# Feature rows beside a group's first tile, a shorter rest before the gates, and another order of the last two groups in a two-layer graph network

## The chip, the cores and the metric

The kernel runs on one core of a Trainium2 chip. The metric is the device time of one execution in microseconds; before the change the median of three runs is 2276.93 us (2276.39 to 2278.49).

The core has five engines with a queue of instructions each, worked through in order: PE (matrix multiplication; PEld are its weight loads), DVE (vector), ACT (scalar and table functions), POOL and SP. In this kernel POOL issues the indirect transfers (gathers and scatters by a list of row numbers), SP and ACT the direct ones.

## The reference

A graph of 6250 nodes with 256 features and 106250 edges, sorted by target, goes through two layers. Each layer adds its result to its input and normalizes the sum.

```python
# layer 0: two small networks, one per kind of edge, on the source's features
h = relu(x[src] @ W_rel[r].T + b_rel[r]); msg = relu(h @ W_rel[r].T + b_rel[r])
agg = segment_sum(msg, dst)
i, f, g, o = split(agg @ W_ih.T + b_ih + b_hh, 4)
hn = sigmoid(o) * tanh(sigmoid(i) * tanh(g))
x = layernorm(x + relu(relu(hn @ W1.T + b1) @ W2.T + b2) @ W3.T + b3)

# layer 1: attention over the incoming edges, four heads of 64; self loops are added to the edges
h = x @ W
e = leaky_relu(a_src[src] + a_dst[dst], 0.2)
alpha = softmax of e over the edges of each target
y = segment_sum(h[src] * alpha, dst) + bias + x
x = layernorm(x + relu(layernorm(y) * gamma + beta))
```

Since the two networks of layer 0 depend on the source node and the kind of edge alone, the kernel computes them once per node and kind and gathers the results.

## The kernel before

**Prologue.** The edge lists are packed so that the self loops fall out, 100000 edges stay and every tile holds 128 of them, 782 tiles (`TC`) in all. Seven tiles make a window, 112 of them (`NW`), which covers at most 64 neighbouring target nodes; two windows make a group, 56 of them (`NG`), whose 128 slots (64 per window) lie on the 128 partitions. The first node of a window is read into SP registers (`lows_of`). The last two windows of the list have no room for 64 whole rows behind their first node, so group 55 moves its own rows by an indirect transfer with the row numbers `tail_x` (reading) or `tail_i` (writing). Both are derived from `tail` (L1105 to L1117), where slots of window 110 that belong to window 111 get a row number outside the nodes, the same for all of them. Then the message networks run (PE, DVE's L1165, ACT's L1168) and their rows are stored in `parts0`.

**Layer 0** (`fast`, first half). A loop over `n` works through the tiles: POOL gathers the 128 message rows of tile `n` (L1646, recorded at L1265 in the helper `gather`), and PE sums tile `n - 4` into the group's accumulator with a one-hot matrix (`sum0`, L1622). With the first tile of a group SP loads the group's self-loop messages (`own_rows`, L1423; a gather on POOL for group 55). Work after the sums is cut into chains, Python generators in `Steps`. After each tile, `run.step()` lets every chain whose rest is over issue its next piece, the older chain first; a `yield k` rests for `k` tiles, a `yield 0` is a `yield 1`. After the last tile `run.finish()` steps until all chains are through. So the rests decide the order in which instructions stand in the engines' queues.

Two chains belong to a group's end. `turn` adds the self loops on DVE (L1433, L1437) and one step later transposes the sums into `faT` (PE L1448, DVE L1451). `update` runs once for four groups, for two near the end, and singly for groups 52 to 55. Its pieces: SP loads the groups' feature rows `xn` (L1461; for group 55 a POOL gather), rest 4, six gate pieces (PE L1475, ACT L1483), tanh (ACT L1492), `hn` (DVE L1495), three layers (L1499 with L1503, L1506 with L1508 and the bias added to `xn` at L1511, L1520 with the residual `xn` at L1522), the normalization (ACT L1529, a square root, which needs another table in ACT than the gates; DVE L1531, L1536), transposition (L1545, L1549), the product with the second layer's weights (PE L1558, ACT L1562 and L1563) and the store into `rows1` (SP L1569; for group 55 the POOL scatter L1571).

**Layer 1** (second half) can gather from `rows1` only when all of it is stored. Its loop over `t` gathers tile `t` (L1930). Per group, `weights` computes the attention scores: a transposition (PE L1750), scans over the edges (DVE L1757, L1758), a product (PE L1761, L1762), two more scans (L1767, L1768), a transposition (PE L1773), and on DVE L1776 to L1779 with ACT's exponential into `ex` (L1781). It then puts the group's pieces into the list `late`: the two windows, and for all groups but 55 one more tile that is shared with the next group. `sum1` takes a piece from `late`, weights its rows on DVE (`weighted`: L1796, ACT L1801, L1802; ahead of a group's first piece the one-hot matrix, L1348), and issues one sum on PE (L1911). In the loop it is called once or twice per tile, from `t = 782` on twice. When a group's sums are issued, the chain `finish` divides and normalizes: DVE L1817 to L1827, L1834 to L1841, then twice the pieces of `normed` (DVE L1849, L1850, ACT L1851, L1852, DVE L1854, ACT L1857), with DVE L1861 to L1863 between. SP stores the rows (L1868), two halves per group, each after the earlier one has landed; group 55 uses the POOL scatter L1870.

Buffers are handed out in rotation by `ring(pool, shape, dtype, name, n)`, `n` being their number.

Of the kernel before, what the change touches and what calls it, by code (L numbers as in the profile page):

```python
# [33 lines left out]
F32 = mybir.dt.float32  # L34
I32 = mybir.dt.int32
AF = mybir.ActivationFunctionType
OP = mybir.AluOpType
# [5 lines left out]
P = 128  # L43
N = 6250
D = 256
# [658 lines left out]
def gnn_kernel(  # L704
# [67 lines left out]
    with (  # L772
# [15 lines left out]
        with (  # L788
# [260 lines left out]
            for to, of in (  # L1049
# [55 lines left out]
            tail = lp.tile([P, 2], F32, name="tail")  # L1105
            lo, hi = slice(0, SLOTS), slice(SLOTS, P)
            nc.vector.tensor_add(tail[lo, 0:1], iota_p[lo], low_b[lo, NW - 2 : NW - 1])
            nc.vector.tensor_scalar(
                tail[lo, 1:2], tail[lo, 0:1], low_b[lo, NW - 1 : NW], float(NP), op0=OP.is_ge, op1=OP.mult
            )  # L1110
            nc.vector.tensor_tensor(tail[lo, 0:1], tail[lo, 0:1], tail[lo, 1:2], op=OP.max)
            nc.vector.scalar_tensor_tensor(
# [83 lines left out]
def fast(  # L1196
# [50 lines left out]
    def windows_of(g):  # L1247
        return range(2 * g, 2 * g + 2)

    def lows_of(ws):  # L1250

        ws = [w for w in ws if w < NW - 2]
        return dict(zip(ws, lows(ws[0], len(ws)))) if ws else {}
# [83 lines left out]
    def ring(pool, shape, dtype, name, n):  # L1337

        of = rings.setdefault((name, id(pool)), [[], 0])
        if len(of[0]) < n:  # L1340
            of[0].append(pool.tile(shape, dtype, name=f"{name}_{len(of[0])}"))
        of[1] += 1
        return of[0][(of[1] - 1) % n]
# [17 lines left out]
    with (  # L1361
# [64 lines left out]

        def turn(g, i, ps, aT):

            agg = ring(up, [P, D], F32, "agg", 3)

            kind = ring(up, [P, 2], F32, "kind", 3)
            for r in range(2):
                nc.vector.tensor_scalar(  # L1433
                    kind[:, r : r + 1], ps[:, D:], float(3 - r), None, op0=OP.is_equal
                )
            for r, of in ((0, ps[:, :D]), (1, agg)):
                nc.vector.scalar_tensor_tensor(  # L1437
                    agg,
                    loop0[g][:, r * D : (r + 1) * D],
                    kind[:, r : r + 1],  # L1440
                    of,
                    op0=OP.mult,
                    op1=OP.add,
                )
            yield 1
            pt = ring(upp, [P, 4 * P], F32, "fpg", 5)[:, : 2 * P]
            for k in range(2):
                nc.tensor.transpose(  # L1448
                    pt[:, k * P : (k + 1) * P], agg[:, k * P : (k + 1) * P], ident
                )  # L1450
            nc.vector.tensor_copy(  # L1451
                aT[:, :, i * P : (i + 1) * P], pt.rearrange("p (k n) -> p k n", k=2)
            )

        def update(groups, aT):
            slow = min(3, max(1, (NG - 4 - groups[0]) // 4))
            cols = len(groups) * P
            at_w = lows_of([w for g in groups for w in windows_of(g)])
            xn = [ring(up, [P, D], F32, "fxn", 8) for g in groups]
            for i, g in enumerate(groups):  # L1460
                own_rows(g, at_w, xn[i], x)  # L1461
            yield 4
            hn = ring(up, [P, 2, 4 * P], F32, "fhn", 2)
            cells = []
            for m in range(2):
# [131 lines left out]
                        nd3[half_of(w), :, :, :].rearrange("p c a h -> p c (a h)"),  # L1597
                    )

        got, ohs, sums, turned, stored, loop0 = {}, {}, {}, {}, [], {}  # L1600
        run.start(weights_of_logits())

        def order_of(g):
# [29 lines left out]
        for n in range(TC + LAG):  # L1633
            if n < TC:
                g, t = order[n]
                k, turns = n % WT, n // WT // 10 % 2
                if k == 0:
                    seven = ring(rowsp, [P, WT * HA], F32, "G", 10).rearrange(
                        "p (j f) -> p j f", f=HA
                    )  # L1640
                    m = min(WT, TC - n)
                    of, to = mark[:, n : n + m, None], seven[:, :, D : D + 1]
                    nc.scalar.copy(to[:, ::-1, :][:, :m, :] if turns else to[:, :m, :], of)

                got[t] = seven[:, WT - 1 - k if turns else k, : D + 1]
                gather(got[t][:, :D], parts0, idx0[:, t : t + 1])  # L1646
                if t == order_of(g)[0]:
                    ohs[g] = ring(ep, [P, 2 * W8, SLOTS], F32, "oh0", 2)
                    one_hot(ohs[g], 2 * g, 2 * W8)
                    loop0[g] = ring(up, [P, 2 * D], F32, "loop0", 2)  # L1650
                    own_rows(g, lows_of(windows_of(g)), loop0[g], loops)
            if n >= LAG:
                g, t = order[n - LAG]
                if t != 2 * WT * g:
                    sum0(g, t, t == TC - 1)
                elif g:
                    sum0(g - 1, t, True)
                if t == 2 * WT * g + WT:
                    sum0(g, 2 * WT * g)
            run.step()  # L1660
# [3 lines left out]
    with (  # L1664
# [72 lines left out]
        def weights(pair, box):  # L1737
# [45 lines left out]
            for i, g in enumerate(pair):  # L1783

                for w in reversed(windows_of(g)):
                    late.append((g, w, i * GS + WT * (w % 2), len(tiles_of(w)[0]), G[w], ex, by(top)))
                if g < NG - 1:
                    late.append((g, w + 2, i * GS + 2 * WT, 1, G[w + 2], ex, by(top)))

        def weighted(g, w, o, n, of, ex, top):  # L1790
# [88 lines left out]
        pair_of = {g: p for p in pairs for g in p}  # L1879
        boxes = {p[0]: {} for p in pairs}  # L1880
        sums, queue, read, ohs, k3s, left, written = {}, [], set(), {}, {}, {}, []

        def sum1():

# [38 lines left out]
        while t < TC + LAG or late or queue or run.chains:  # L1923
            if t < TC:
                w = t // WT
                if t % WT == 0:
                    G[w] = ring(rowsp, [P, WT * HA], F32, "G", 10).rearrange(
                        "p (j f) -> p j f", f=HA
                    )
                gather(G[w][:, t - WT * w, :], rows1, idx1[:, t : t + 1])  # L1930
            k = t - LAG
            if 0 <= k < TC:
                w = k // WT
                g = w // 2
                pair = pair_of[g]
                box = boxes[pair[0]]
                if k % (2 * WT) == 0:
                    if g == pair[0]:
                        box["e"] = ring(ep, [P, 2 * GS, H], F32, "e", 3)
                    if g:  # L1940

                        old = pair_of[g - 1]
                        ob = boxes[old[0]]
                        nc.scalar.copy(  # L1944
                            ob["e"][:, old.index(g - 1) * GS + 2 * WT, :], G[w][:, 0, D:HA]
                        )
                        if old is not pair:
                            run.start(weights(old, ob))
                if k == tiles_of(w)[0][-1]:
                    o = pair.index(g) * GS + WT * (w % 2)  # L1950
                    own = len(tiles_of(w)[0])
                    nc.scalar.copy(box["e"][:, o : o + own, :], G[w][:, :own, D:HA])
                    if w == NW - 1:
                        run.start(weights(pair, box))
            sum1()
            if len(queue) + W8 * len(late) > 3 * W8 or t % 7 == 0 or t >= TC:
                sum1()
            run.step()
            t += 1

# [61 lines left out]
```

## Time and profile before

| what | us |
|---|---|
| median of three runs | 2276.93 |
| the profiled execution | 2273.88 |
| its span, first to last instruction | 2271.7 |
| first gather of layer 0 | 203.70 |
| last gather of layer 0 | 1190.38 |
| first gather of layer 1 | 1220.96 |
| last gather of layer 1 | 2205.13 |
| last scatter | 2259.47 |
| busy: PE, DVE, ACT, POOL | 1550.3, 1235.5, 506.9, 1526.7 |

A row of the timeline has the start and the duration in us, the engine, the line, the operation, what it writes and reads, how often, and in brackets how long the engine had been idle and what ended that. A row of a group has its number of instructions, busy time and mean duration in ns, and the idle time ahead of them by what ended it. "q" behind an engine's name stands for its queue (issuing a transfer, waiting for a semaphore).

### The profile page before, as it was taken

To read this page: it belongs to the slowest core of one execution; us is meant where nothing else is said; L and a number is where in the kernel's file an instruction comes from. 1 tells how busy PE (TensorE), PEld (TensorE's weight loads), DVE (VectorE), ACT (ScalarE), POOL (GpSimd) and SP (SyncE) were. 2 spreads that over 40 slices of the span, in tenths; PEclk is the share of its full clock that TensorE was granted. 3 is DMA by queue.
4 is the path that set the end of the run, shared out by engine and by line. 5 is a ranking of instruction groups with operands and counts; after the bars stand their busy time and mean duration, and the time that the engine had idled before them with its cause. 6 is when DMAs were issued, how large, how long until landed. Compare 5 with 4: busy or idle time off the path is not lost. (4 is left out here: it accounts for less than half of the span.)

```text
span 2271.7 us, 22029 instructions
## 1 busy us (share of the span) xinstructions
PE 1550.3 (68%) x5722; PEld 769.7 (34%) x5722; DVE 1235.5 (54%) x3332; ACT 506.9 (22%) x1525; POOL 1526.7 (67%) x1603
## 2 busy tenths in 40 slices
PE   8987688888988888888992354554545555355564
PEld 5654233333333333333451232322323223232232
DVE  7452133333333343333542577677776877777786
ACT  3322022221222212222342112211111111212111
POOL 1213777777777777777774777777777777777760
PEclk9988899999999999999996676766767666676776
DMA  5335435554555555555553555555555555555550
GB/s 160 123 95 152 132 115 168 165 159 144 144 168 165 157 149 144 168 164 164 172 163 93 143 156 149 155 144 158 151 147 162 144 157 151 148 160 146 151 145 24
DMA packets 163393, 332.53 MB, mean 146 GB/s; under 512 B 42451, under 2 KB 74290, under 8 KB 163257
## 3 DMA queue, kind: packets, MB, share of 16 engines
q0 software_dynamic: 75968, 208.00, 33.9%
q1 hardware_dynamic: 64736, 82.92, 11.4%
q10 hardware_dynamic: 22553, 40.12, 5.8%
q8 instruction: 47, 0.77, 0.1%
q14 instruction: 89, 0.73, 0.1%
HBM read 278.79 MB, written 52.12 MB: 146 GB/s over the span
## 5 line engine op out<-in xcount | busy, mean ns | idle before, releaser
L1265 POOL DMA_INDIRECT G<-parts,fidx x782 | 748.5, 957 | 305.7 <-issue 218.4
L1265 POOL DMA_INDIRECT G<-rows,fidx x782 | 747.3, 956 | 240.6 <-issue 221.1
L1622 PE MATMUL fps<-G,oh 128*64 128x257 f32 (+1 forms) x1674 | 523.4, 425 | 149.2 <-DMA G<-parts,fidx 142.4
L1911 PE MATMUL fps<-gw,oh 128*64 128x264 f32 (+1 forms) x1674 | 440.0, 475 | 230.8 <-DVE gw L1802 230.6
L1911 PEld LDWEIGHTS fps<-gw,oh 128*64 128x64 f32 (+1 forms) x1674 | 231.3, 169 | 408.8 <-DVE gw L1802 247.6
L1622 PEld LDWEIGHTS fps<-G,oh 128*64 128x64 f32 (+1 forms) x1674 | 191.9, 147 | 457.4 <-DMA G<-parts,fidx 241.5
L1802 DVE TENSOR_TENSOR gw<-G,bank 128x1792 f32<-128x1792 f32 (+1 forms) x167 | 248.9, 1490 | 178.0 <-ACT gw L1801 174.9
L1433 DVE TENSOR_SCALAR kind<-fps 128x1 f32<-128x1 f32 x112 | 12.5, 152 | 308.5 <-PE fps L1622 308.5
L1475 PE MATMUL fpg<-faT,fWihT 128*128 128x512 f32 (+2 forms) x432 | 172.4, 524 | 0.0
L1750 PE MATMUL turn<-fident,e 128*120 128x128 f32 (+2 forms) x30 | 13.7, 457 | 223.6 <-ACT e L1944 223.6
L1348 DVE TENSOR_TENSOR oh<-bank,fslot 128x1024 f32<-128x1024 f32 x112 | 135.9, 1213 | 2.2 <-ACT bank L1781 2.2
L1583 DVE COPY nd<-hr 128x4 f32<-128x4 f32 x56 | 10.9, 194 | 162.6 <-ACT hr L1562 162.6
L1851 ACT ACTIVATE frs<-fmv,eps_c 128x1 f32<-128x1 f32 x112 | 33.0, 294 | 297.0 <-DVE fmv L1850 147.1
L1143 PE MATMUL fph<-fxc,fWrT 128*128 128x512 f32 (+1 forms) x208 | 92.7, 595 | 6.5 <-DMA fWrT<-in_WrT_dram 6.4
L1475 PEld LDWEIGHTS fpg<-faT,fWihT 128*128 128x128 f32 x432 | 72.1, 194 | 68.8 <-issue 58.9
L931 POOL DMA_INDIRECT packed<-frame,place x21 | 20.9, 993 | 108.2 <-DVE fms L1165 70.8
L1857 ACT ACTIVATE fy<-fy,frs 128x256 f32<-128x256 f32 x112 | 67.2, 600 | 100.2 <-DVE gw L1796 55.1
L1157 PE MATMUL fpm<-fWrT,fhT 128*128 128x256 f32 x392 | 89.0, 380 | 0.6 <-DVE fms L1165 0.5
L1750 PEld LDWEIGHTS turn<-fident,e 128*120 128x120 f32 (+2 forms) x30 | 5.0, 168 | 238.0 <-ACT e L1944 236.0
L1801 ACT COPY gw<-bank 128x28 f32<-128x28 f32 (+1 forms) x167 | 28.4, 170 | 228.5 <-DMA dB<-slots 101.3
L1157 PEld LDWEIGHTS fpm<-fWrT,fhT 128*128 128x128 f32 x392 | 73.3, 190 | 17.7 <-issue 5.0
L1165 DVE TENSOR_TENSOR fms<-fpm,fbrr 128x512 f32<-128x512 f32 x49 | 33.6, 687 | 76.1 <-PE fpm L1157 74.9
(236 smaller groups left out, 1817.8 us busy)
## 6 DMA issues: line engine op xcount, KB each, us to landing
kept<-keep SPq DMA_DIRECT2D x56, 384.0 KB
k<-kept ACTq DMA_DIRECT2D x56, 384.0 KB
dB<-slots ACTq DMA_DIRECT2D x112, 128.0 KB
loop<-parts SPq DMA_DIRECT2D x110, 128.0 KB
parts<-fms SPq DMA_DIRECT2D x49, 256.0 KB
G<-parts,fidx POOLq DMA_INDIRECT x782
G<-rows,fidx POOLq DMA_INDIRECT x782
rows<-hr SPq DMA_DIRECT2D x110, 65.0 KB
```

The lines of the kernel that those rows point to most:

```text
L1143: nc.tensor.matmul(ph[:, :cols], WrT_s[:, r, k, m * P : (m + 1) * P], xc[:, k, :cols], start=(k == 0), stop=(k == 1),)
L1157: nc.tensor.matmul(pm[:, r, :], hT[:, r, k, j * P : (j + 1) * P], WrT_s[:, r, k, :], start=(k == 0), stop=(k == 1),)
L1165: nc.vector.tensor_add(ms.rearrange("p r f -> p (r f)"), pm.rearrange("p r f -> p (r f)"), brr)
L1265: nc.gpsimd.indirect_dma_start(out=to_tile, out_offset=None, in_=table, in_offset=bass.IndirectOffsetOnAxis(ap=idx, axis=0),)
L1348: nc.vector.tensor_tensor(to[:, :nj, :], iota_s[:, None, :].to_broadcast([P, nj, SLOTS]), of[:, :, None].to_broadcast([P, nj, SLOTS]), op= ...
L1475: nc.tensor.matmul(pg[:, :cols], WihT_s[:, k, c * P : (c + 1) * P], aT[:, k, :cols], start=(k == 0), stop=(k == 1),)
L1622: nc.tensor.matmul(sums[g][to, :], ohj, got[t], start=begins, stop=ends)
L1801: nc.scalar.copy(gw[:, :, D:HA], ex[:, o : o + n, :])
L1802: nc.vector.tensor_mul(gw[:, :, :D].rearrange("p j (h f) -> p j h f", h=H), of[:, :n, :D].rearrange("p j (h f) -> p j h f", h=H), ex[:, o ...
L1851: nc.scalar.activation(r, mv[u, k, 1:2], AF.Ln, bias=eps_c[u])
L1857: nc.scalar.activation(y, y, AF.Identity, bias=m, scale=r)
L1911: nc.tensor.matmul(sums[g][to, :], ohj, gw, start=begins, stop=ends)
```

## The change

```diff
             nc.vector.tensor_add(tail[lo, 0:1], iota_p[lo], low_b[lo, NW - 2 : NW - 1])
-            nc.vector.tensor_scalar(
-                tail[lo, 1:2], tail[lo, 0:1], low_b[lo, NW - 1 : NW], float(NP), op0=OP.is_ge, op1=OP.mult
+            nc.vector.tensor_scalar(tail[lo, 1:2], iota_p[lo], float(NP + SLOTS), None, op0=OP.add)
+            nc.vector.scalar_tensor_tensor(
+                tail[lo, 1:2],
+                tail[lo, 0:1],
+                low_b[lo, NW - 1 : NW],
+                tail[lo, 1:2],
+                op0=OP.is_ge,
+                op1=OP.mult,
             )
...
         def turn(g, i, ps, aT):
-            agg = ring(up, [P, D], F32, "agg", 3)
+            agg = ring(up, [P, D], F32, "agg", 2)
...
         def update(groups, aT):
...
-            xn = [ring(up, [P, D], F32, "fxn", 8) for g in groups]
-            for i, g in enumerate(groups):
-                own_rows(g, at_w, xn[i], x)
-            yield 4
+            xn = [rows_x[g] for g in groups]
+            yield 2
...
                     loop0[g] = ring(up, [P, 2 * D], F32, "loop0", 2)
-                    own_rows(g, lows_of(windows_of(g)), loop0[g], loops)
+                    rows_x[g] = ring(up, [P, D], F32, "fxn", 9)
+                    at_w = lows_of(windows_of(g))
+                    own_rows(g, at_w, loop0[g], loops)
+                    own_rows(g, at_w, rows_x[g], x)
...
         def weights(pair, box):
...
-                if g < NG - 1:
+                if g == NG - 1:
+                    weighed.append(g)
+                else:
                     late.append((g, w + 2, i * GS + 2 * WT, 1, G[w + 2], ex, by(top)))
...
-            sum1()
-            if len(queue) + W8 * len(late) > 3 * W8 or t % 7 == 0 or t >= TC:
+
+            if t >= TC + LAG and not weighed:
+                run.step()
+            else:
                 sum1()
+                if len(queue) + W8 * len(late) > 3 * W8 or t % 7 == 0 or t >= TC:
+                    sum1()
             run.step()
```

- The slots of window 110 that belong to window 111 get row numbers outside the nodes that differ from each other.
- The feature rows of a group are loaded with its first tile, after its self-loop rows, into one of nine buffers (before: eight); the sums with self loops have two buffers (before: three).
- `update` begins with a rest of 2.
- From `t = 786` on (`TC + LAG`), until `weights` of group 55 has put its pieces into `late`, the loop issues no sums and steps the chains twice. The sums of group 54 that are not issued by then (all but its first two) follow after that.

More of the change, by code (lines that the diff above doesn't have):

```diff
@@ L1598, in update @@
                     )
-        got, ohs, sums, turned, stored, loop0 = {}, {}, {}, {}, [], {}
+        got, ohs, sums, turned, stored, loop0, rows_x = {}, {}, {}, {}, [], {}, {}
         run.start(weights_of_logits())
@@ L1881, in fast @@
         sums, queue, read, ohs, k3s, left, written = {}, [], set(), {}, {}, {}, []
+        weighed = []
         def sum1():
```

## The prediction

> **What bounds the kernel now.** I read the page's groups first, then the POOL rows of the timeline, then the two stretches in which POOL has nothing to do.
>
> ```profile
> L1265 POOL DMA_INDIRECT G<-parts,fidx x782 | 748.5, 957 | 305.7 <-issue 218.4 <-ACT G L1643 67.8 <-PE fps L1622 7.6
> L1265 POOL DMA_INDIRECT G<-rows,fidx x782 | 747.3, 956 | 240.6 <-issue 221.1 <-DMA G<-rows,fidx 5.8 <-PE fps L1911 1.2
> ```
>
> Each layer is 782 gathers on POOL, 0.95 us busy and 0.30 us of issue apart, so one every 1.25 us. Between 203.7 and 1191.3 us, and again between 1221.0 and 2206.2, POOL waits for no engine worth naming. PE, in contrast, waits for the gathers (142 us of L1622's idle time is "DMA G<-parts"). So nothing that shifts PE, DVE, ACT or SP inside a layer can move the end. What counts is the prologue, the boundary of the layers (last gather 1190.38 to first gather of the second layer 1220.96) and the tail after the last gather (2205.13).
>
> The boundary, from the timeline (start, duration, instruction):
>
> ```profile
> 1191.64 0.94 POOL L1265 DMA_INDIRECT fxn<-in_x_dram,tail_x  x1 [0.30 <-issue]
> ...
> 1194.53 0.22 DVE L1433 TENSOR_SCALAR kind<-fps 128x1 f32<-128x1 f32 x2 [1.71 <-PE fps L1622]
> ...
> 1198.13 1.22 PE L1520 MATMUL fpg<-fW3T,fz 128*128 128x256 f32 x2 [0.46 <-ACT fz L1508]
> ...
> 1201.48 1.28 ACT L1529 ACT_TABLE_LOAD   x1
> ...
> 1217.27 1.00 POOL L1571 DMA_INDIRECT rows<-hr,tail_i  x1 [24.69 <-ACT keep L1563]
> ```
>
> The x rows land early (they are first needed at L1511, 1208.38). The time goes into the chain sums, turn, gates, three small layers and norm of group 55, in one instruction stream with that of group 54: PE reaches the first gate of 55 (L1475, 1199.14) only behind 54's L1520, and ACT swaps its table for 54's square root between 55's second and third gate.
>
> The tail, from the timeline:
>
> ```profile
> 2238.79 0.21 ACT L1781 ACTIVATE bank<-e 128x48 f32<-128x48 f32 x1 [0.29 <-DVE e L1779]
> ...
> 2242.97 7.75 PE L1911 MATMUL fps<-gw,oh 128*128 128x264 f32 x24 [6.74 <-DVE gw L1802]
> ...
> 2250.75 0.16 DVE L1817 TENSOR_TENSOR sm<-loop,fps 128x4 f32<-128x4 f32 x1 [0.59 <-PE fps L1911]
> ...
> 2259.47 1.00 POOL L1870 DMA_INDIRECT out_dram<-fy,tail_i  x1 [53.28 <-POOLq L1182]
> ```
>
> Scores of 55 (ready 2238.79), one-hot and two products on DVE, twelve sums, then the normalizations alone, 8.72 us from L1817 to the last scatter. Between 2236 and 2243 DVE is busy 6.50 of 7 us (busy time by stretch), so here DVE is the engine that decides.
>
> **The change, part by part.** *Padding rows* (L1108): one DVE instruction becomes two, 0.20 us more (L1108's own row) at 161 us. The first gather (203.70) waits for ACT's L1643, and that for the messages' stores, which hang on PE's L1157 (DVE's L1165 waits 74.9 us for it); 0. Without that cover, +0.2. A sentence apart: the Trainium skill ("DMA: Bandwidth & Descriptors", Rules for kernel authors) says that every duplicate in a scatter still goes out as a write of its own, so distinct targets would save no write; no run here shows it, and it changes no term.
>
> *x rows with the first tile.* Per group the same two SP loads (469 ns each), now straight behind the two self-loop loads. On SP they pass the stores of older groups, 0.94 us later for those, which nobody waits for before the boundary. The ninth buffer is free in time: its reader, L1522 of the group nine earlier, ran many tiles before. POOL is the exception: group 55's x rows are a gather, which moves from after the last gather to ahead of eleven of them. Those come 1.25 us later, and so does L1433 of group 55: 1194.53 to 1195.78.
>
> *Rest 2 in place of 4.* Counted in the code, all later steps of every update come two tile steps earlier. Inside the layer that is hidden under POOL (cost without cover: PE's waits for faT, about 0.4 us a quad). At the boundary both 54 and 55 shift by two, so their interleaving from the first gate on is unchanged, table loads included. What changes: 54's L1499 falls into the step of the last sum. Before it waited for L1495 and started at 1196.11; now it follows the sums, which ended at 1194.49 and now at 1195.74. From there to L1520 it is 2.02 us (1196.11 to 1198.13): 1197.76, which is 0.37 earlier. 55's turn goes between: its transposes follow 54's L1506 (1195.74 + 1.07 + 0.49 = 1197.30), then 0.41 and the copy 0.42, so faT is ready by 1198.17, ahead of L1520's end (1197.76 + 1.01 = 1198.77). First gate 1198.77 against 1199.14, and everything behind it the same: **-0.37 us**. Bounds: if only faT held the gate (1198.30), -0.84; if the earlier steps gained nothing, the whole gather stands, +1.25.
>
> *The end.* From t = 786 the sums of 54 are held and the steps run twice per turn until 55's weights are queued. On DVE that takes two things out of the way of 55's scores: the one-tile product (2231.95 to 2232.34, with the gap at its end 0.36) and 54's L1817/L1819 (0.27). Scores at 2238.16, **0.63 earlier**. But 53's L1857 now stands before the one-tile product on ACT: it starts 2238.30, holds ACT for 0.51 (2229.03 to 2229.54 in the row before), the copy 0.14, so that product starts at 2238.99. From there, by start-to-start distances of the same rows: 0.33 to the one-hot, 1.13, 0.33, 1.40, 0.33, 1.94 to the first instruction of 54's finish: 2244.45, against 2245.10 for the DVE instruction that followed the last product.
>
> Now 54's finish, which used to lie under the products and sums, stands ahead of 55's, six steps before it. I laid both out on DVE and ACT in the new order with the distances of the rows after 2250.75 (0.455 us for dependent operations of 256, about 0.34 for independent ones, Ln and Exp 0.5, L1857 0.60): 55's L1817 can start 4.32 us after 2244.45, at 2248.77; its gamma step waits for two L1857 in a row; the scatter comes 15.02 us after 2244.45, at 2259.47. The 0.65 is given back exactly: **0**.
>
> PE: the sums of 54 restart at 2235.15, behind the last transposition of 55's scores. The clock decides:
>
> ```profile
> 2227.70:2231.10 3.40, 3.40 (x9) 1.35 (x8) 2.77 (x9) 0.74 (x3) 0.00 (x0) 0.50 0.41 129
> 2231.10:2234.50 3.40, 3.40 (x19) 2.07 (x19) 3.23 (x12) 0.47 (x3) 0.00 (x0) 0.90 0.09 21
> ```
>
> (window, length, then PE, PEld, DVE, ACT, POOL busy with counts, clock, DMA.) Sums that began at 2226.71 ran at 0.50 for 4.4 us, 0.88 us each, then 0.42 each; those from 2242.97 took 5.2 us to speed up. So 13 sums of 54: 4.4 to 5.2 us slow (5.0 to 5.9 sums), the rest fast, to 2242.9 to 2243.3; twelve of 55 end at 2248.0 to 2248.4, before 2248.77. No cost, with 0.4 us of room. Apart from that sum, a rule against the change: the Trainium skill ("TensorE: Matmul & The Clock Gate", Part 1: The HAM clock gate) has a free-running window of about 3.4 us and half clock after an idle one, so up to two windows can be slow; with 6.8 us my estimate is an end at 2249.2, and the sum would be 0.4 us higher.
>
> The new wait: 54's rows go out after its last L1857, which stands behind 55's first Ln and Exp: it ends at 2255.25 (before, 2251.84). SP issues two halves, the second after the first has landed: 1.94 us (2252.65 to 2254.59) to 3.58 (2245.91 to 2249.49) later. POOL's semaphore rows for the last scatter begin 2.05 us after the second (2256.64) and take 0.38, then 0.2 to the scatter: 2259.85 to 2261.5. I take 2.5, the mean of the last four pairs: 2260.4, **+0.9**. Queued behind it is the end of the program alone. Ends: -0.65 (54's finish holds nothing up) and +2.0.
>
> **Sum.** -0.37 + 0 + 0.9 = +0.5 us. The profiled execution took 2273.88 (span 2271.7 and 2.2 around it) and would take 2274.4; the median of the runs lies 3.05 higher, so 2276.93 + 0.5 gives **2277.5 us**.
>
> **The rivals.** *Faster: both rests and the waiting were on the path.* Two tile steps are 2.5 us. 55's scores take 8.07 us (2230.72 to 2238.79), of which its own instructions are 4.04 (DVE 2.97, PE 0.92, ACT 0.15); with nothing between, 4.0 less. -6.5: **2270.4**. For it: 6.74 us of PE idle. Against: DVE's 6.50 of 7 us, and 53's finish stays in the stream. 0.12.
>
> *Slower: the sums run at the slow clock throughout.* 25 sums of 0.88 from 2235.15 end at 2257.2, 8.4 after the 2248.77 at which they begin to decide; with the boundary +8.0: **2284.9**. For it: PE does little between 2229 and 2235. Against: 0.90 after one full window. 0.12.
>
> *It removes nothing*: x rows and rest were hidden and the earlier gather remains, +1.25, the end even: **2278.2**, within 0.2%. 0.20.
>
> **From these to the numbers.** Forecast 0.56. About 0.2% (4.6 us) is what a measurement of this kernel can tell from no change. Faster 0.12, within 0.76, slower 0.12. Range: low ends -0.84 - 0.65 and the 0.5 by which a run lay under the median, rounded down, 2274.6; high ends +1.25 + 2.0 and some of the 1.6 above it, 2281.0.
>
> **What will show it.** Boundary: x gather second after group 55's first tile; L1433 about 1.25 us after its old distance to the layer's start; L1499 of 54 straight behind the sums; both table loads still between L1483's second and third gate; first gather near 1220.6. Tail: scores 0.6 earlier, PE without a break from L1773 to the last sum, 54's L1861 between 55's L1819 and L1823, the scatter behind SP's L1868. Wrong if PE's last sum ends after the DVE is ready for it, if a table load falls away, or if POOL's distance of 1.25 us changes.

## The result, and the profile after

The changed kernel takes 2284.78 us (median of 7 runs, 2284.04 to 2287.13), the kernel before 2277.36 in the same comparison (7 runs, 2273.44 to 2279.91). The ratio is 1.0037, with a 95% interval of 1.0027 to 1.0047: slower by 7.4 us between the medians, where 0.5 us and "within 0.2%" were forecast. The profiled execution took 2286.02 us, its span is 2284.2. The two profiled executions lie further apart than the medians, because the one before was 3.5 us under its median and this one is 1.2 over.

The page's groups for the changed kernel show the loss at once. The columns are those of the prediction: count, busy time, mean ns, idle time ahead.

```profile
L1271 POOL DMA_INDIRECT G<-parts,fidx x782 | 759.1, 971 | 305.7 <-issue 218.4
L1271 POOL DMA_INDIRECT G<-rows,fidx x782 | 746.6, 955 | 240.7 <-issue 219.6
```

The same 782 gathers of layer 0 are busy 759.1 us instead of 748.5. Their idle time has not moved (305.7 both times). POOL does not wait longer between gathers; some gathers themselves take longer. The whole difference of the two spans (2284.24 - 2271.73 = 12.51 us), from the rows of POOL:

| stretch | before | after | difference | forecast |
|---|---|---|---|---|
| start to first gather | 203.70 | 204.87 | +1.17 | 0 |
| first to last gather of layer 0 | 986.68 | 998.55 | +11.87 | +1.25 (the moved gather of x) |
| last gather to first gather of layer 1 | 30.57 | 28.47 | -2.10 | -1.62 (1.25 moved away, 0.37 gained) |
| first to last gather of layer 1 | 984.17 | 983.60 | -0.57 | 0 |
| last gather to last scatter | 54.34 | 56.49 | +2.15 | +0.9 |
| scatter to the end of the span | 12.26 | 12.26 | 0 | 0 |

10.6 of the 11.87 are the busy time above, 1.25 the moved gather. The timeline of the changed kernel shows which gathers are long. A row with "x3" stands for three instructions in a row, from the first one's start to the last one's end; rows of the other engines are left out.

```profile
732.24 0.95 POOL L1271 DMA_INDIRECT G<-parts,fidx  x1 [0.30 <-issue]
732.80 1.28 DVE L1499 TENSOR_TENSOR fhn<-fgg,fgo 128x512 f32<-128x512 f32 x2
733.49 1.41 POOL L1271 DMA_INDIRECT G<-parts,fidx  x1 [0.30 <-issue]
...
753.01 0.95 POOL L1271 DMA_INDIRECT G<-parts,fidx  x1 [0.30 <-issue]
753.91 1.08 DVE L1555 TENSOR_TENSOR keep<-keep,fbias 128x256 f32<-128x256 f32 x3
754.26 1.56 POOL L1271 DMA_INDIRECT G<-parts,fidx  x1 [0.30 <-issue]
756.12 0.95 POOL L1271 DMA_INDIRECT G<-parts,fidx  x1 [0.30 <-issue]
```

A gather takes 0.95 us, except where a DVE operation on two SBUF operands is under way at its start (or, in the row of L1540 below, one on a single SBUF operand). It then takes longer by the time to the end of that DVE work, less 0.13 us: the three additions end at 754.99, that is 0.73 after 754.26, and 1.56 is 0.61 more than 0.95. The product `fhn` ends at 734.08, 0.59 after 733.49, and 1.41 is 0.46 more. DVE work that starts after a gather does nothing to it, unless the gather is already held, as by the third addition here. In the changed kernel 72 gathers are long (over 0.965 us), and 71 of them end 0.82 us after the end of such an operation, to within 0.02 us; the other is the first of the layer. Counting the gathers that start under the two-operand operations of the table (begun more than 0.03 us before, more than 0.15 us left of it): 48 of 50 are long in the profile before, 48 of 48 in the changed kernel's.

The kernel has a counterexample of its own. The one-hot comparison (L1348, L1354 after the change) takes about 1.2 us, longer than any of them, and has two operands too, but one of them, the row of numbers in `bank`, lies in PSUM. By the same count 50 gathers start under it in the profile before and 37 in the changed kernel's, and none is long.

For a sum, I took from every gather of layer 0 what it lasts beyond 0.946 us, and gave it to the DVE operation whose end explains it (us; the last row is over all 782 gathers and lies below the sum of the others because some take 0.942):

| operation | before | after |
|---|---|---|
| `keep` + bias, L1551 / L1555 | 1.1 | 6.8 |
| `fhn`, L1495 / L1499 | 2.4 | 5.0 |
| `fgg` times `fgi`, L1488 / L1492 | 3.0 | 3.5 |
| `xn` + `b3r`, L1511 / L1515 | 1.3 | 2.9 |
| second `agg`, L1437 / L1443 | 1.1 | 0.6 |
| `keep` normalized, L1536 / L1540 | 0.3 | 0.8 |
| all gathers | 8.7 | 19.3 |

Each quad of groups has four additions of the bias, in the changed kernel three back to back and the fourth some 10 us later; from one quad to the next are some 71.6 us, and the gathers come 1.25 us apart. In the changed kernel eleven quads have the second and third addition at the same place over a gather's start, and each of the eleven costs 0.60 to 0.61 us. So the operations are the same ones, in the same number and at the same durations. Only where they lie against the starts of the gathers has changed.

The boundary in the changed kernel, from its timeline:

```profile
1189.66 0.95 POOL L1271 DMA_INDIRECT fxn<-in_x_dram,tail_x  x1 [0.30 <-issue]
...
1207.85 0.23 DVE L1439 TENSOR_SCALAR kind<-fps 128x1 f32<-128x1 f32 x2 [2.43 <-PE fps L1626]
...
1209.86 0.70 PE L1524 MATMUL fpg<-fW3T,fz 128*128 128x256 f32 x2 [0.24 <-ACT fz L1512]
...
1211.87 1.28 ACT L1533 ACT_TABLE_LOAD   x1
...
1228.18 1.00 POOL L1575 DMA_INDIRECT rows<-hr,tail_i  x1 [23.80 <-ACT keep L1567]
```

The gather of x now stands ahead, the rest runs as before, and the scatter comes 24.75 us after the last gather (1203.43) instead of 26.88.

The tail, from the same timeline; the first row is the exponential of group 53, three from the last:

```profile
2215.84 0.22 ACT L1788 ACTIVATE bank<-e 128x60 f32<-128x60 f32 x1 [0.36 <-DVE e L1786]
...
2249.76 0.21 ACT L1788 ACTIVATE bank<-e 128x48 f32<-128x48 f32 x1 [0.29 <-DVE e L1786]
...
2253.91 5.60 PE L1921 MATMUL fps<-gw,oh 128*128 128x264 f32 x24 [0.28 <-DVE gw L1811]
...
2260.33 0.15 DVE L1826 TENSOR_TENSOR sm<-loop,fps 128x4 f32<-128x4 f32 x1
...
2271.98 1.00 POOL L1879 DMA_INDIRECT out_dram<-fy,tail_i  x1 [55.54 <-POOLq L1188]
```

And PE there by stretch (window, length, then PE, PEld, DVE, ACT, POOL busy with counts, clock, DMA):

```profile
2246.50:2249.90 3.40, 3.40 (x11) 1.99 (x12) 2.74 (x11) 1.00 (x4) 0.00 (x0) 0.50 0.00 0
2249.90:2253.30 3.40, 3.40 (x18) 1.94 (x15) 2.57 (x4) 0.81 (x4) 0.00 (x0) 0.77 0.08 19
```

The held-back sums of group 54 run at half clock for the first 5 us, from 2246.50 to about 2251.5 (forecast 4.4 to 5.2), and the last sum is over at 2259.51, before DVE reads it (2260.33). PE does not decide.

### The profile page after: what moved, and what is told of

Same layout as the page of the kernel before. It is cut to its first block, busy times and chain, and to the rows that moved or that the text cites. A ratio compares the mean times of both kernels' runs of the same rounds, so it can differ in the third digit from the quotient of the medians.

```text
span 2284.2 us, 22013 instructions
## 1 busy us (share of the span) xinstructions
PE 1557.0 (68%) x5722; PEld 769.6 (34%) x5722; DVE 1233.0 (54%) x3333; ACT 505.0 (22%) x1525; POOL 1536.6 (67%) x1603
## 5 line engine op out<-in xcount | busy, mean ns | idle before, releaser
L1271 POOL DMA_INDIRECT G<-parts,fidx x782 | 759.1, 971 | 305.7 <-issue 218.4
L1757 PE MATMUL turn<-fident,e 128*120 128x128 f32 (+2 forms) x30 | 13.7, 457 | 222.1 <-ACT e L1954 222.1
L1354 DVE TENSOR_TENSOR oh<-bank,fslot 128x1024 f32<-128x1024 f32 x112 | 136.2, 1216 | 3.2 <-ACT bank L1788 3.2
L1492 DVE TENSOR_TENSOR fgg<-fgg,fgi 128x512 f32<-128x512 f32 (+2 forms) x36 | 20.6, 573 | 143.2 <-ACT fgg L1487 143.2
L1757 PEld LDWEIGHTS turn<-fident,e 128*120 128x120 f32 (+2 forms) x30 | 5.0, 168 | 236.4 <-ACT e L1954 235.2
L1526 DVE TENSOR_TENSOR keep<-fpg,fxn 128x256 f32<-128x256 f32 x56 | 23.7, 423 | 104.5 <-PE fpg L1524 98.2
```

What stands on the lines that cost most here:

```text
L1271: nc.gpsimd.indirect_dma_start(out=to_tile, out_offset=None, in_=table, in_offset=bass.IndirectOffsetOnAxis(ap=idx, axis=0),)
L1354: nc.vector.tensor_tensor(to[:, :nj, :], iota_s[:, None, :].to_broadcast([P, nj, SLOTS]), of[:, :, None].to_broadcast([P, nj, SLOTS]), op= ...
L1526: nc.vector.tensor_add(y, p3[u, :], xn[i])
```

## The experiments

Theory A: DVE operations on two SBUF operands hold the gathers, and the rest of 2 moved them onto gather starts. Theory B: the early loads of feature rows disturb the gathers. Theory C: the new end costs it. Eighteen kernels were run in five groups, each group on one chip with the kernel before beside it.

**One warning on two of the five chips.** There the medians of all kernels, the one before too, were 3054 to 3083 us. The first group (e) and the third (g) fell on such chips. What waits there can be seen in the list of waits of e3_end (engine, line and what ended the wait, where "remote" is no instruction of the core; us, times, longest):

```profile
DVE s L1757 <- remote: 451.3, 24, 20.8
```

In the profile before, the longest wait of L1757 is 5.3 us. L1757 belongs to layer 1. There POOL waits some 20 us (once 42) in 25 of the 28 pairs of groups, and in layer 0 too its gathers have more idle time ahead of them than in the profile before (467 us against 306). So POOL does not set the time alone on these chips, and a change of a gather's length need not show in it. What makes the waits long there was not settled. Ratios of these two groups are read for their sign at most.

**First group: rests and parts, on such a chip.** e1_rest4 is the changed kernel with the old rest, e2_rest2 the kernel before with the new one, e3_end the kernel before with the new end alone, e4_noadds the changed kernel with the two additions of constants taken off DVE.

```diff
# e1_rest4 (changed kernel)        # e2_rest2 (kernel before)
-            yield 2               -            yield 4
+            yield 4               +            yield 2
# e4_noadds
-                nc.vector.tensor_add(xn[i], xn[i], b3r)
-                nc.vector.tensor_add(keep3[i][u, 1, :], y, bias_r[u, :])
+                nc.scalar.copy(keep3[i][u, 1, :], y)
```

> The changed kernel with the rest of 4 put back; x rows at the first tile and the new end stay. Theory A (a DVE operation with two operands in SBUF that is under way when a gather starts on POOL holds that gather until it ends, and the rest of 2 moved such operations onto the starts): the busy time of layer 0's gathers falls from 759 us to 747 to 751 (before: 748.5), and the time is 0 to 3 us above that of before, against 7 to 8 for the change. Rival B (the x loads, moved to every group's first tile, disturb the gathers): the gathers stay at 757 to 761 us and the time 6 us or more above. Rival C (the end costs it all): gathers either way, time 6 us or more above.

> The kernel before with the rest of 2 and nothing else changed; the x loads stay at the start of update. Theory A: the busy time of layer 0's gathers rises from 748.5 to 756 to 761 us, the time is 6 to 10 us above before, nearly all of the change's loss. Rival B: gathers at 747 to 751 us, time within 2 us. Rival C: time within 2 us.

> The kernel before with the new order of the last two groups alone. Theory A: gathers of layer 0 at 748 to 750 us as before; from the last gather to the last scatter 56.0 to 56.7 us in place of 54.3 (the change had 56.5), so 1.5 to 2.5 us above before in all. Rival C: 6 us or more above.

> The changed kernel without b3 (L1515 left out, so the first layer's result lacks b3) and with the addition of bias, which is zero here, replaced by a copy on ACT (L1555): the two DVE operations behind which 9.8 us of the gathers' delay lie (2.9 and 6.9) are gone. Theory A: busy time of layer 0's gathers 747 to 753 us, time 6 to 11 us below the changed kernel, so within 4 us of before. Rivals B and C: gathers stay at 757 to 761 us, time at most 2 us below the changed kernel.

Measured: e1_rest4 0.9956 (0.993 to 0.9983), gathers of layer 0 751.9 us; e2_rest2 1.0061 (1.0033 to 1.0089), 754.2 us; e3_end 0.9998 (0.9965 to 1.0031), 752.1 us; e4_noadds 1.005 (1.0026 to 1.0075), 747.8 us. The rest of 2 costs without any other part of the change, which speaks against B and C. The sizes are not those of A: e2_rest2 is some 20 us above the kernel before, forecast were 6 to 10, with gathers only 2.3 us longer than e1_rest4's, and the gathers of e1_rest4, e2_rest2 and e3_end lie outside A's ranges by 1 to 2 us. e4_noadds missed most: its gathers are as short as A said, its time is not. From first to last gather of layer 0 it takes 1247 us for 978 us of gathers and their issue (782 x 1.25), so on this chip something else sets the layer's pace, and the run says nothing on the time.

**Second group: the decisive one, on a chip with a kernel before of 2276.48 us.** The same two kernels again, the changed kernel with its two constants in PSUM, and the mechanism by itself.

```diff
# f3_psum (changed kernel); every ring "fpg" has 4 tiles in place of 5
+        held = upp.tile([P, 2, D], F32, name="held")       # PSUM
+        nc.scalar.copy(held[:, 0, :], b3r)
+        nc.scalar.copy(held[:, 1, :], bias_r)
-                nc.vector.tensor_add(xn[i], xn[i], b3r)
+                nc.vector.tensor_add(xn[i], xn[i], held[:, 0, :])
-                nc.vector.tensor_add(keep3[i][u, 1, :], y, bias_r[u, :])
+                nc.vector.tensor_add(keep3[i][u, 1, :], y, held[u, 1, :])
```

> The changed kernel with a rest of 4 instead of 2 ahead of the gates (early feature rows and the new end kept), measured again because in the first four runs every kernel, the one before too, took about 3060 us. Theory A (DVE operations with two inputs in SBUF, under way when a gather of layer 0 starts, hold that gather; the rest of 2 moved them onto gather starts): the gathers of layer 0 are busy 748 to 752 us instead of 759.1, the ratio to before is 0.998 to 1.001. Theory B (the early loads of the feature rows disturb the gathers): they stay at 757 or more, ratio 1.003 or more. Theory C (the end costs it): gathers as in the changed kernel's second layer, ratio 1.003 or more with the last gather to the scatter at 56.5 us against 54.3.

> The kernel before with nothing changed but the rest of 4, now 2 (feature rows still loaded at the update, old end). Theory A: the gathers of layer 0 take 755 to 760 us instead of 748.5 and the ratio to before is 1.002 to 1.005. Theory B or C: no part of what they blame is in this kernel, so 748 to 750 us and a ratio within 0.999 to 1.001.

> The changed kernel with the two constant rows that two DVE additions of the update read (b3 and the second layer's bias) copied once into PSUM, and the ring of gate tiles 4 instead of 5 to make the bank free. The additions are the same, at the same place, but have one input in SBUF. Theory A: what these two held (6.9 and 2.9 us of 19.3) goes, the gathers of layer 0 take 749 to 751 us and the ratio to before is 0.998 to 1.000; the other two-input operations still hold gathers. Theory B or C, or any account by the order of the work alone: gathers at 757 or more, ratio 1.003 or more.

> A kernel that measures the disputed cost alone: stages of 40 gathers of 128 rows of 256 f32 into free buffers on POOL, and beside each stage nothing, or one kind of DVE operation back to back: an addition of 128x512 with both inputs in SBUF, the same with one input in PSUM, a multiplication by a constant (one input), an addition of two SBUF inputs into PSUM, an addition of 128x256 with two SBUF inputs, a copy on ACT, a scalar_tensor_tensor of 128x256 with two SBUF inputs. The computation of the reference is left out, its time stands for nothing. Theory A: gathers are 0.95 us alone, beside the operations with one SBUF input and beside ACT; beside two SBUF inputs they are longer by the rest of the operation under way at their start less 0.13 us, that is about 0.2 to 0.3 us on average at 0.68 us an operation and 0.1 at 0.43 us, and no gather is longer by more than one operation. Rival: any DVE operation that writes SBUF holds them (then all the DVE stages but the one that writes to PSUM are longer), or none does (all 0.95 us).

f1_rest4: 2276.36 us, ratio 1.0002 (0.9993 to 1.0011). f2_rest2: 2282.18 us, 1.0032 (1.0019 to 1.0044). f3_psum: 2274.76 us, 0.9992 (0.9982 to 1.0001). The gathers of layer 0 on the three pages, in this order:

```profile
L1271 POOL DMA_INDIRECT G<-parts,fidx x782 | 749.1, 958 | 306.0 <-issue 223.4
```

```profile
L1265 POOL DMA_INDIRECT G<-parts,fidx x782 | 758.2, 970 | 305.5 <-issue 220.9
```

```profile
L1271 POOL DMA_INDIRECT G<-parts,fidx x782 | 747.9, 956 | 305.9 <-issue 287.6
```

One digit of the kernel before, a 2 for a 4, makes the loss; the same digit taken back in the changed kernel unmakes it. f3_psum keeps the rest of 2 and has the three additions at nearly the same place. Its timeline, one of the eleven quads:

```profile
324.87 1.07 DVE L1559 TENSOR_TENSOR keep<-keep,held 128x256 f32<-128x256 f32 x3
325.23 0.95 POOL L1271 DMA_INDIRECT G<-parts,fidx  x1 [0.30 <-issue]
```

Set this beside 753.91 and 754.26 above: the three additions again start some 0.35 us ahead of a gather, and the gather takes 0.95, not 1.56. In this profile 39 gathers start under one of the two additions that now read PSUM, and none takes over 0.96 us. So it is neither the time of the additions nor DVE being busy; it is that both operands come from SBUF. (The ring of four tiles in place of five was not run by itself; what shows the cause is that the gathers over these additions are no longer held.)

f4_micro, from its timeline: additions of two SBUF tiles (L132), additions with one operand in PSUM (L134), and multiply-adds of two SBUF tiles (L137).

```profile
63.60 0.68 DVE L132 TENSOR_TENSOR to_two<-a,b 128x512 f32<-128x512 f32 x1
63.87 1.24 POOL L156 DMA_INDIRECT G<-in_x_dram,idx_two  x1 [0.30 <-DVE tu_two L132]
...
121.62 0.68 DVE L134 TENSOR_TENSOR tu_psum_in<-ps,b 128x512 f32<-128x512 f32 x1
121.65 0.95 POOL L156 DMA_INDIRECT G<-in_x_dram,idx_psum_in  x1 [0.30 <-issue]
...
408.84 0.47 DVE L137 SCALAR_TENSOR_TENSOR to_stt<-a,iota_p,b 128x256 f32<-128x256 f32 x1
408.85 29.39 POOL L156 DMA_INDIRECT G<-in_x_dram,idx_stt  x1 [0.30 <-issue]
...
436.95 0.47 DVE L137 SCALAR_TENSOR_TENSOR tu_stt<-a,iota_p,b 128x256 f32<-128x256 f32 x1
```

Of 40 gathers that start under an addition with one operand in PSUM, none is longer than 0.95 us; neither is one of the 24 under ACT's copies alone, and of 172 with nothing under way on DVE and ACT one takes 0.97. Under an operation on two SBUF operands, counted as above (begun more than 0.03 us before, more than 0.15 us left of it), 26 of 27 are held (of the 16 whose result goes to PSUM, all), and nearly all of them last to its end and 0.82 us more, 0.946 less 0.13. In the 27th the operation had begun only 0.06 us earlier, and it took longer itself (0.52 in place of 0.47). That count leaves out near ties: sixteen gathers start within 0.01 us after one addition of two SBUF tiles began, with 0.07 to 0.08 us left of the addition before it. None of them is held; the addition takes 0.72 us in place of 0.68 instead. The eleven long ones of the kernel start 0.02 us after an addition began and are held. Who wins close to a tie was not settled. Two points went against what I expected of A. The multiplication by a constant, with one SBUF operand, holds gathers as well: 24 of 24, by 0.19 us on average. It runs at 0.41 us for the 512 elements that an addition takes 0.68 for. And a gather can be held for more than one operation: the last one shown waits 28.44 us, through a whole run of back-to-back multiply-adds, until it ends (437.42 - 408.85 - 0.13 = 28.44).

The order in the stages was not the one planned (part of the gathers ran ahead of their stage), so only gathers with a known DVE operation at their start are counted, and stage means are not used.

**Third and fourth group: what the end and the early rows cost, and the mechanism put to use.** The end alone (as e3_end); the changed kernel with rest 4 and the old end (early rows alone); the kernel before, and the changed one with rest 4, with three operations turned to one SBUF operand: the two of f3_psum and the second multiply-add of `turn`, whose first now writes back into its PSUM accumulator.

```diff
-            for r, of in ((0, ps[:, :D]), (1, agg)):
+            for r, to in ((0, ps[:, :D]), (1, agg)):
                 nc.vector.scalar_tensor_tensor(
-                    agg,
+                    to,
...
-                    of,
+                    ps[:, :D],
```

On the second of the 3070 us chips:

> The kernel before with the new end alone (the last group's weights ahead of the sums of the one next to it). The stretch from the last gather to the scatter was 54.3 us in the profile before, 56.5 in the changed kernel, but also 56.7 in f2_rest2, which has the old end, and 55.3 in f1_rest4, which has the new one. Theory A (the loss is in layer 0 alone, the end is worth nothing that can be told): ratio to before 0.999 to 1.001, the stretch between 54 and 58 us. Theory C (the new end costs the 2 us by which the stretch grew): ratio 1.0005 to 1.0015, the stretch at 56 to 57.

> The changed kernel with a rest of 4 and the old end: what is left of the change is the early load of the feature rows, their ring of 9, two buffers for agg instead of 3 and the longer sum of the last index. Theory A: gathers of layer 0 busy 748 to 751 us as in f1_rest4 (749.1), ratio 0.999 to 1.001. Theory B (early loads cost): 752 or more, ratio 1.002 or more.

> The kernel before, nothing of the change in it, with b3 and the bias held in PSUM (gate ring 4 instead of 5), and the first of turn's two multiply-adds written back into its PSUM tile, so that the second has one input in SBUF. Theory A: of the 8.7 us by which the gathers of layer 0 were longer than 0.946 each, these three operations account for 3.4; the gathers take 744 to 747 us instead of 748.5 and the ratio is 0.997 to 0.9995. A theory in which only the order of the work counts: no difference, 0.9995 to 1.001.

> The changed kernel with a rest of 4, b3 and bias in PSUM and the multiply-add written back into PSUM. From f1_rest4 (9.3 us over 0.946 a gather in layer 0), b3, bias and agg account for 3.4 us. Theory A: the gathers of layer 0 take 744.5 to 747 us, the ratio is 0.997 to 0.9995, and no gather is held by these three operations any more; if the early loads or the end are worth something of their own, it is lower than g3_b_psum by that.

Ratios 1.0011 (0.9986 to 1.0036), 0.9972 (0.9951 to 0.9994), 1.0004 (0.9977 to 1.0032) and 1.0004 (0.9982 to 1.0026), gathers of layer 0 752.4, 751.0, 748.2 and 748.4 us: nothing to decide by. The same four on a chip with a kernel before of 2277.74 us:

> The kernel before with the new end alone, as g1_end, asked again because the chip of g1_end took 3070 us for every kernel. Theory A (the loss is in layer 0 alone): ratio 0.999 to 1.001, gathers of layer 0 747 to 750 us, last gather to scatter anywhere from 54 to 58 us. Theory C (the new end costs the 2 us that this stretch grew by): ratio 1.0005 to 1.0015 and the stretch 56 to 57 us.

> The changed kernel with a rest of 4 and the old end, as g2_early: early loads alone. Theory A: gathers of layer 0 748 to 751 us, ratio 0.999 to 1.001, and h1_end, h2_early and f1_rest4 can't be told apart from before. Theory B (early loads cost): 752 us or more, ratio 1.002 or more.

> The kernel before with b3 and bias in PSUM and the first multiply-add written back into PSUM, as g3_b_psum, where none of the three operations held a gather any more, while the gathers held by the gates' product went from 5.1 to 5.6 us. Theory A: gathers of layer 0 744 to 747 us, ratio 0.997 to 0.9995.

> The changed kernel with a rest of 4 and the same three operations with one input in PSUM, as g4_best. Theory A: gathers of layer 0 744.5 to 747 us, ratio 0.997 to 0.9995.

| kernel | median us | ratio (95%) | gathers of layer 0, us | beyond 0.946 each, us |
|---|---|---|---|---|
| h1_end | 2280.22 | 1.0011 (1.0002 to 1.0020) | 749.2 | 9.4 |
| h2_early | 2276.58 | 0.9995 (0.9986 to 1.0004) | 746.8 | 7.1 |
| h3_b_psum | 2274.30 | 0.9982 (0.9973 to 0.9991) | 744.9 | 5.1 |
| h4_best | 2275.85 | 0.9989 (0.9980 to 0.9998) | 745.1 | 5.3 |

The early rows cost nothing that can be told (0.9995, 0.9986 to 1.0004): B falls. The new end's kernel is slower by 0.2 to 2 in a thousand, at the upper edge of what A allowed. Not all of that need be the end: the profile of h1_end has 3.4 us more than the profile before at the boundary, which the new end does not touch. From the exponential of group 53 to the scatter, the timelines of h1_end (new end) and h2_early (old end):

```profile
2208.39 0.22 ACT L1781 ACTIVATE bank<-e 128x60 f32<-128x60 f32 x1 [0.31 <-DVE e L1779]
...
2264.54 1.00 POOL L1872 DMA_INDIRECT out_dram<-fy,tail_i  x1 [57.34 <-POOLq L1182]
```

```profile
2205.12 0.22 ACT L1788 ACTIVATE bank<-e 128x60 f32<-128x60 f32 x1 [0.30 <-DVE e L1786]
...
2260.57 1.01 POOL L1877 DMA_INDIRECT out_dram<-fy,tail_i  x1 [56.03 <-POOLq L1188]
```

56.15 against 55.45 us. Over the eleven profiles on the 2277 us chips this stretch is 56.08 to 56.20 with the new end (five kernels) and 54.65 to 55.45 with the old one (six): about 1 us. Measured from the last gather it scatters between 54.3 and 58.9, because the exponential itself comes between 0.9 us before and 2.8 us after that gather. So the 2.15 us of the first table are 0.9 of the end and 1.25 of where the chain of group 53 happened to stand.

In h3_b_psum and h4_best the three turned operations hold no gather any more, and what is left is nearly all `fgg` and `fhn`. h3_b_psum is faster than the kernel before.

**Fifth group: the boundary.** With a rest of 2 throughout, last gather to first gather of layer 1 took 28.5, 29.0 and 29.7 us (changed kernel, f2_rest2, f3_psum), with a rest of 4 30.6 to 33.9. If the last group's rest does it, it should do so with that group alone:

```diff
-            yield 4
+            yield 2 if groups[-1] == NG - 1 else 4
```

> The kernel of h3_b_psum (no early rows, old end, three operations with one input in PSUM) with the rest of 2 for the update of the last group alone and 4 for all others. Theory A (a shorter rest costs only where gathers run, and gains where they have ended): gathers of layer 0 744 to 746.5 us as in h3_b_psum (744.9), the stretch from the last gather of layer 0 to the first of layer 1 29 to 30.5 us instead of 31.8, ratio to before 0.9965 to 0.9985. If the shorter stretch in the kernels with a rest of 2 throughout (28.5, 29.0, 29.7) had another cause, it stays at 31 to 32 and the ratio at 0.998.

> The changed kernel with the early rows, the old end, a rest of 2 for the last group's update alone, and the three operations with one input in PSUM. Theory A: gathers of layer 0 744.5 to 747 us, the stretch between the layers 28 to 30 us (no gather of x in it), ratio 0.9965 to 0.9985, not slower than k1_last2 by more than the gather of x (1.25 us) that now stands among layer 0's.

k1_last2: 2273.22 us, 0.9984 (0.9975 to 0.9993), stretch 31.8 us. k2_last2: 2273.90 us, 0.9986 (0.9977 to 0.9995), stretch 31.9 us. The stretch has not moved, so the last group's rest alone does not shorten it. In k1_last2 the last input gate of group 55 is through ACT 4.5 us sooner after the last gather than in h3_b_psum (11.3 against 15.8), but the first `fhn` only 2.0 (17.05 against 19.04) and the scatter none (28.04 against 28.05). Group 55 waits behind the chain of group 54, which keeps the rest of 4: in k1_last2 its first layer (PE L1503) starts only behind 54's L1562.

```profile
1200.86 2.13 PE L1562 MATMUL fpg<-Wx,fyT 128*128 128x264 f32 x4 [2.48 <-ACT fyT L1553]
...
1201.05 0.49 DVE L1499 TENSOR_TENSOR fhn<-fgg,fgo 128x128 f32<-128x128 f32 x2 [1.86 <-ACT fgg L1496]
...
1202.79 1.06 PE L1503 MATMUL fpg<-fhn,fW1T 128*128 128x128 f32 x4
```

The page of k2_last2 has the shortest gathers of all:

```profile
L1271 POOL DMA_INDIRECT G<-parts,fidx x782 | 740.9, 947 | 305.9 <-issue 288.8
```

Only 1.2 us beyond 0.946 each are left, against 5.3 in h4_best with the same layer 0 but for the last group's rest. `fgg` cost 2.0 there and 0.1 here: where the operations fall against the gathers differs even between such near kernels. k1_last2, k2_last2 and h3_b_psum can't be told apart; each is faster than both kernels of this study.

## Why the prediction was wrong

The step that failed is the sentence "So nothing that shifts PE, DVE, ACT or SP inside a layer can move the end", and with it the costing of the rest of 2 inside the layer: "Inside the layer that is hidden under POOL". I read from POOL's idle time that it waits for no engine, which is right and stayed right (305.7 us both times), and took its busy time for a constant. It isn't. In the profile before, 57 of the 782 gathers already lasted over 0.965 us, 8.7 us in all beyond 0.946 each, which the mean of 957 ns gave away. Two tile steps less of rest moved DVE's work against the starts of the gathers: 72 long ones, 19.3 us, that is 10.6 us more, put at nothing in the sum. The last of the prediction's own signs of being wrong, "if POOL's distance of 1.25 us changes", is the one that came. f2_rest2 shows the cost by itself (1.0032), f1_rest4 that without it nothing is lost (1.0002), f3_psum why.

The Trainium skill has the rule that I left out, in "SBUF — State Buffer", section "Who interferes with whom": DVE and GpSimd share a pair of SBUF ports under an exclusive lock, and a `tensor_tensor` with both inputs in SBUF contends with GpSimd's reads. The runs agree (0 of 40 held with one operand in PSUM, 26 of 27 with two in SBUF). The same section infers that such an operation does not keep a transfer's descriptors from being written; the gathers here, which are transfers issued by POOL, were held, and the measurement decides. It also has whoever comes first keep the pair for one whole instruction; here DVE kept it through several (28.44 us in f4_micro).

Point by point:

- **The end, chain 0 and wait +0.9.** From the exponential of group 53 to the scatter 55.24 became 56.14, which is +0.90. 55's L1826 comes 4.29 us after 54's (2260.33 - 2256.04; forecast 4.32), SP's second half is issued at 2268.74 and POOL's semaphore rows begin 2.06 later (2.05). 55's scores, counted from the exponential of group 53, come 0.64 us earlier (forecast 0.63), and the half clock lasted 5 us of the sums, inside the forecast. The end came out in its parts and in its sum, and h1_end's 0.2 to 2 thousandths agree.
- **The boundary, -0.37 net.** -0.85 net by the table above. In f2_rest2, where the gather of x stays behind, the stretch is 1.61 us shorter than in the profile before; the same working without the moved gather gives 1.62 (0.37 and 1.25). The order was right: first gate behind L1524, the table load where it was. k1_last2 fits it: 55's own rest alone gains nothing, because 55 waits for 54's chain. That the sizes come so close is partly luck: two kernels with the same boundary, the one before and h1_end, have 30.57 and 33.94 us there, so one profile can't size a term of this kind to less than 3 us.
- **The prologue, 0.** The first gather is 1.17 us later in the profile after. Over the eleven profiles it starts between 201.2 and 205.1 us, with and without the longer sum, so nothing can be told of it.
- **Early rows.** Cost hidden, as forecast: h2_early 0.9995.
- **The rivals.** The slower rival named 2284.9 us, near the 2284.78 measured, by a mechanism that did not occur (25 sums at half clock). The faster one did not occur either. None had the mechanism that decided.
- **Slips of the sums.** 2238.30 + 0.51 + 0.14 is 2238.95 (the text has 2238.99), 1197.30 + 0.41 + 0.42 is 1198.13 (1198.17), and the low end of the range comes to 2274.9 (2274.6). None bears on the miss.

The sum of the parts measured alone: rest 1.0032, end 1.0011, early rows 0.9995, together 1.0038; measured 1.0037. Each of the three is known to about a thousandth, so that the two agree this closely is luck; that the rest makes up most of it is not.

## What to carry to other kernels

Where POOL issues indirect transfers one behind another and sets the time, look at the spread of their durations before calling the other engines hidden: a mean above the shortest says that something holds them. DVE operations on two SBUF operands (and some on one) beside them cost by where they fall, which any change of order shuffles; putting one of the two operands in PSUM took the cost away wherever they fell in these runs. A new order should then be judged by several kernels that differ a little, since one alignment may lose or win several us by chance.

## What was not expected of the hardware

- With back-to-back operations a gather can be held through all of them (28.44 us in f4_micro, the second and third of three additions in the kernel), so the hold does not end with each operation.
- A one-operand multiplication of 128x512 in SBUF at 0.41 us holds gathers as two-operand additions do (24 of 24). In the kernel L1540, with one SBUF operand of 128x256 and 0.41 us, holds 10 of 12 in the profile after, while the statistics of the normalization (L1528), also with one, hold none of 25. What tells the one-operand operations apart was not settled.
- In the microbenchmark DVE gives way as well: an addition that starts together with a gather takes 0.72 us instead of 0.68, and the gather is not held.
- Two of five chips took 3054 to 3083 us for kernels that take 2273 to 2285 on the others; why stays open.
